# Moving sums and a broadcast ahead of preparation products in TensorE's order in a selective-scan layer

## The chip, the cores and the metric

The kernel runs on one core of a Trainium2 chip. The metric is the device time of one launch in microseconds (us), the median of a few runs. The core has five engines with a queue each: TensorE (PE, matmuls; its weight loads are listed as PEld), VectorE (DVE), ScalarE (ACT), GpSimd (POOL) and SyncE (SP, which here issues nearly all transfers). Each runs its own list of instructions and waits on semaphores for the others. A smaller time is better.

## The reference

Four layers are applied to an image batch of 3 x 256 x 48 x 48 in float32, each as `x = x + layer(group_norm(x))`: an attention block, a convolution with routed weights, a plain 3 x 3 convolution, and a selective scan (Mamba) layer. The change is in the scan layer alone. For every batch and token it computes, cut to what matters:

```python
xn = layer_norm(x)                          # over the 256 channels
u  = silu(causal_conv4(in_proj_x(xn)))      # 512 channels
z  = in_proj_z(xn)                          # 512 channels
dt_raw, B, C = split(x_proj(u), [16, 16, 16])
dt = softplus(dt_proj(dt_raw))
h  = h * exp(dt * A) + dt * B * u           # 512 channels x 16 states, token after token
y  = sum_over_states(h * C) + u * D
out = out_proj(y * silu(z))
```

## The kernel before

The 2304 tokens of each of the three batches are cut into six chunks of 384 tokens (`CH`), so the scan layer has 18 chunks (`todo`), taken one after the other. A chunk has 512 x 16 = 8192 rows of state, which are run as eight **steps** (m, h): m = 0..3 names a block of 128 channels, h = 0, 1 the half of the states. A step has eight **parts**, each a scan of 128 rows over 384 tokens. Part p of a step is written "p0" to "p7" below, with the step before it: (1,0) p3.

What one part does: ACT computes `exp(A * dt)` into one of three PSUM slots (`decay`, L1758), and DVE runs the recurrence in place over a buffer `hs` (`scan`, L1766). The decay of a part is issued three parts ahead, into the slot that the scan just listed has freed. So ACT can be at most three parts ahead of DVE, and whatever else is listed on ACT between two decays delays those behind it.

What a step needs besides: the buffer `hs` is filled with `dt * B * u` beforehand, the upper half by DVE from PSUM (`fill_upper`, L1719), the lower by POOL from SBUF (`fill`, L1733). After the step's eight scans, POOL multiplies the states by C (`times_c`, L1783), and one step later PE sums them over the states into the PSUM tile `ps_y` (`add_states`: eight matmuls of 32 columns, L1800, and with h = 0 one matmul with the diagonal of D ahead of them, L1795, which opens a new `ps_y`). `gate` on DVE (L1807) multiplies the finished `ps_y` by silu(z). It stands at the end of step (m,1) for block m-1, and `ps_y` has one buffer, so the opening matmul of `add_states` at the end of (m,1) needs that gate. `dt * u` reaches the scans in two ways: `spread_pe` (L1689, four listed matmuls) broadcasts it over partitions into the PSUM tile `ps_r`, which has one buffer and is read by `fill_upper`; `spread` reads it and dt back from DRAM through SP's queue into the SBUF tiles `dtur` and `dtr`.

Beside the scans of chunk `at`, the next chunks are prepared. This work is laid out by hand in the table `plan`: an entry (j, place, rel, stage) puts a stage of chunk at + rel into half-step j = 0..15 of chunk `at` (j = 4m + 2h, plus 1 for parts 4 to 7). The places are points in the order of listing: MID after the second part of the half-step, DONE after the third, LATE after the fourth, and PE_ for TensorE's products: for an even j after part p3, for an odd j after the whole step. `keep_order` makes PE, DVE, ACT and POOL execute exactly in the order of listing.

The preparation shares two PSUM banks (`bank[0]`, `bank[1]`), and its order is:

- j = 0, 1, 3, 4 (PE_): `taps` 0 to 3, the products of the convolution, 16 matmul instructions each (L1264), into banks 0, 1, 0, 1; `take_u` (ACT, L1273) empties them at MID of j = 2, 3, 5, 6.
- j = 3 and j = 7 (LATE): `silu` of z and of u on ACT, each with a table load before and after (L1278, L228).
- j = 5 and 6 (PE_): `project_y` 0 and 1 of the chunk before (L1353, L1355); `store` (ACT copy L1365, then a DMA) empties bank 0 at j = 6 LATE and bank 1 at j = 8 MID.
- j = 7 (PE_): `project_u` (L1284); j = 8 LATE: `take_dbc`.
- j = 8 and 10 (PE_): `project_dt` 0 and 2 (L1310); j = 9 and 11 LATE: `softplus` on ACT (L1319 to L1321); j = 10 and 12 MID: `take_dt` (four DVE instructions in place over the two banks and into `dtu`, L1326, L1327); j = 10 and 12 DONE: `keep_dt` (two ACT copies, L1331, that empty the banks, and two DMAs to DRAM).
- j = 12 (PE_): `less_mean` (L1222) of the chunk after the next; j = 13 LATE: `centre` (L1235, L1237); j = 13 (PE_): `square_mean` (L1229); j = 14 MID: `inverse_root` (L1241, L1242); j = 15 MID: `normalise` (DVE, L1246).
- j = 13 to 15 (PE_): `project_z` (L1341), emptied by `take_z` (ACT, L1349).

At the end of a step the list on PE was so far: the odd half-step's preparation product, then `add_states` of the step before, then, with h = 0, `spread_pe` for the step after the next.

Of the kernel before, what the change touches and what calls it, by code (L numbers as in the profile page):

```python
# [9 lines left out]
F32 = mybir.dt.float32  # L10
# [6 lines left out]
P = 128  # L17
# [8 lines left out]
CH = 384  # L26
# [57 lines left out]
def net(  # L84
# [295 lines left out]
    with ExitStack() as l0:  # L380
# [36 lines left out]
        with ExitStack() as p1:  # L417
# [15 lines left out]
            for b in ORDER:  # L433
# [3 lines left out]
                for ct in range(CT):  # L437
                    for j in range(parts):
                        at = slice(j * N // parts, (j + 1) * N // parts)
# [754 lines left out]
    def fetch(at):  # L1194
        k = chunks[at] = Chunk()
        k.at = at
        k.b, k.c = todo[at]
        k.before = chunks.get(at - 1)
        k.xg = room(k, "xg")
        nc.sync.dma_start(k.xg, xd[k.b][:, :, k.c * CH : (k.c + 1) * CH])  # L1200
# [106 lines left out]
    def project_dt(k, m0):  # L1307
        for j in range(2):
            m = m0 + j
            nc.tensor.matmul(  # L1310
                bank[j], w3v["dtsb"][:, m * P : (m + 1) * P], k.dbc[: DTR + 1, :],
                start=True, stop=True,
            )

    def softplus(k, m0):

        both = k.dt[:, m0 : m0 + 2, :]
        for j in range(2):
            nc.scalar.activation(k.dt[:, m0 + j, :], bank[j], AF.Abs)  # L1319
        nc.scalar.activation(both, both, AF.Exp, scale=-1.0)  # L1320
        nc.scalar.activation(both, both, AF.Ln, bias=1.0)  # L1321

    def take_dt(k, m0):
        for j in range(2):
            m, pdt = m0 + j, bank[j]
            nc.vector.scalar_tensor_tensor(pdt, pdt, 0.0, k.dt[:, m, :], ALU.max, ALU.add)  # L1326
            nc.vector.tensor_tensor(k.dtu[:, m, :], pdt, k.u[:, m, :], ALU.mult)  # L1327

    def keep_dt(k, m0):
        for j in range(2):  # L1330
            nc.scalar.copy(k.dt[:, m0 + j, :], bank[j])  # L1331
        if m0 == 0:
            k.dtd, k.dtud = {}, {}
        d = k.dtd[m0] = dram.tile([P, 2, CH], F32, name=f"dtd{m0}")
        nc.sync.dma_start(d, k.dt[:, m0 : m0 + 2, :])
        d = k.dtud[m0] = dram.tile([P // 2, 2, CH], F32, name=f"dtud{m0}")
        nc.sync.dma_start(d, k.dtu[P // 2 :, m0 : m0 + 2, :])
# [13 lines left out]
    def project_y(k, mo, lo=0, hi=DI):  # L1351
        if lo == 0:
            nc.tensor.matmul(bank[mo], ident, k.ot[:, mo, :], start=True, stop=False)  # L1353
        for m in range(lo, hi):
            nc.tensor.matmul(  # L1355
                bank[mo], w("out", m * 256 + mo * P, P), k.sz[:, m, :],
                start=False, stop=m == DI - 1,
            )
# [5 lines left out]
    def store(k, mo):  # L1364
        nc.scalar.copy(k.ot[:, mo, :], bank[mo])  # L1365
        nc.sync.dma_start(
            out[k.b, mo * P : (mo + 1) * P, k.c * CH : (k.c + 1) * CH], k.ot[:, mo, :]
        )
# [3 lines left out]
    MID, DONE, LATE, PE_ = range(4)  # L1372
# [18 lines left out]
        (8, LATE, 1, take_dbc),  # L1391
        (8, PE_, 1, lambda k: project_dt(k, 0)),
        (9, LATE, 1, lambda k: softplus(k, 0)),
        (10, MID, 1, lambda k: take_dt(k, 0)),
        (10, DONE, 1, lambda k: keep_dt(k, 0)),
        (10, PE_, 1, lambda k: project_dt(k, 2)),
        (11, LATE, 1, lambda k: softplus(k, 2)),
        (12, MID, 1, lambda k: take_dt(k, 2)),
        (12, DONE, 1, lambda k: keep_dt(k, 2)),
    ]  # L1400

    after = [
# [2 lines left out]
        (3, LATE, 0, lambda k: silu(k.sz)),  # L1405
        (2, MID, -1, residual),
        (5, PE_, -1, lambda k: project_y(k, 0)),
        (6, LATE, -1, lambda k: store(k, 0)),
        (6, PE_, -1, lambda k: project_y(k, 1)),
        (8, MID, -1, lambda k: store(k, 1)),  # L1410
    ]
# [10 lines left out]
    def run(at, j, place):  # L1422
        for when, where, rel, stage in after + plan + gating:
            if (when, where) == (j, place) and 0 <= at + rel < len(todo):
                stage(chunks[at + rel])
# [230 lines left out]
    with ExitStack() as l3:  # L1656
# [5 lines left out]
        scn = l3.enter_context(tc.tile_pool(name="scn", bufs=2, reuse_waits="tile"))  # L1662
# [10 lines left out]
        def spread(k, m):  # L1673

            dtr = scn.tile([P, 4, CH], F32, name="dtr")
            dtur = scn.tile([P, 2, 16 + CH], F32, name="dtur")[:, :, 8 : 8 + CH]
            for t, src in ((dtr, k.dtd), (dtur, k.dtud)):
                src = src[m & 2][:, m & 1, :]
                for i in range(4):
                    r = slice(32 * i, 32 * i + 32)  # L1680
                    nc.sync.dma_start(t[r], src.rearrange("(q d) n -> d q n", d=32))
            return dtr, dtur

        def spread_pe(k, m):

            t = psr.tile([P, 2, 512], F32, name="ps_r")
            for q in range(2):
                r = slice(32 * q, 32 * q + 32)
                nc.tensor.matmul(  # L1689
                    t[:, q, :CH], rep[r].rearrange("p r d -> p (r d)"), k.dtu[r, m, :],  # L1690
                    start=True, stop=True,
                )
            k.ps = t
# [69 lines left out]
        def scan(s, part):  # L1763
            g, q = parts_of_step[part]
            b = tiles[s][:, g, q, :]
            nc.vector.tensor_tensor_scan(  # L1766
                b, slots[(8 * s + part) % 3][:, : CH + 1], b, 0.0, ALU.mult, ALU.add
            )
# [42 lines left out]
        k = chunks[0]  # L1811
# [6 lines left out]
        for s, (at, m, h) in enumerate(steps):  # L1818
            if m == 0 and h == 1 and at + 2 <= last:
                fetch(at + 2)  # L1820
            for part in range(8):
                j = 4 * m + 2 * h + part // 4
                scan(s, part)
                decay(8 * s + part + 3)
                if part == 0 and h == 0:
                    c, n = (at, m + 1) if m + 1 < DI else (at + 1, 0)
                    if c <= last:
                        rows = getattr(chunks[c], "rows", {})
                        chunks[c].rows = {**rows, n: spread(chunks[c], n)}
                if part == 4 and s + 1 < len(steps):  # L1830
                    first_states(s + 1)
                if part % 4 == 1:
                    run(at, j, MID)
                if part % 4 == 2:
                    run(at, j, DONE)
                if h == 1 and part == 7 and s >= 3:
                    gate(*steps[s - 3][:2])
                if part % 4 == 3:
                    run(at, j, LATE)
                if part == 3:  # L1840
                    run(at, j, PE_)
            if s + 1 < len(steps):
                fill(s + 1)
            last_states(s)
            times_c(s)
            run(at, 4 * m + 2 * h + 1, PE_)
            if s >= 1:
                add_states(s - 1)

            if h == 0 and s + 2 < len(steps):  # L1850
                spread_pe(chunks[steps[s + 2][0]], steps[s + 2][1])

        end = len(steps) - 1
        k = chunks[last]
# [122 lines left out]
```

## Time and profile before

| What | Value |
|---|---|
| median of three runs | 3452.4 us (3451.87 to 3458.52) |
| profiled execution, time | 3452.73 us |
| its span | 3451.2 us |
| scans, first to last start | 2025.8 to 3428.7 us |
| busy over the span: PE, DVE, ACT, POOL | 90%, 85%, 68%, 41% |
| granted TensorE clock, mean | 0.944 |

The scan stage fills the last two fifths of the span. POOL is nearly idle before it and nearly always busy in it, so its 41% says little; the stage is to be read by itself. One chunk takes 78.5 us there, and the order repeats from chunk to chunk: `normalise` is at 2650.26 us in one chunk and at 2728.69 us in the next. Within a line of the timeline the columns are the start in us, the length in us, engine, source line, operation, output and inputs, how many instructions were merged, and in brackets the idle time ahead of them with what ended it. Neighbouring instructions of one engine overlap a little in these records (a scan lasts 0.93 us but follows the one before after 0.85 us), so distances between starts are used where a queue is counted.

### The profile page before, as it was taken

The page shows a single profiled execution, that of the slowest core. Times are in us where ns is not written, and L with a number is a line of the kernel's source. Part 1 is how long each engine was busy: PE and PEld are TensorE (multiplying, and loading weights), DVE is VectorE, ACT ScalarE, POOL GpSimd, SP SyncE. Part 2 cuts the span into 40 slices and gives each one's busy share as a digit, 9 for nine tenths or more (in the row PEclk, how much of TensorE's full clock was granted, in tenths as well). Part 3 has the DMA queues.
Part 4 walks back from the last instruction along what each step waited for, and adds up shares of the span by engine and source line. Part 5 has one row for each costly group of instructions (what it writes and reads, how often), then busy time and mean ns, then how long its engine had stood idle before and what let it go on. Part 6 is the DMA issues. An engine that isn't in the chain of part 4 may idle for free. (4 is left out here: it accounts for less than half of the span.)

```text
span 3451.2 us, 51999 instructions
## 1 busy us (share of the span) xinstructions
PE 3115.5 (90%) x20170; PEld 1496.8 (43%) x20170; DVE 2937.4 (85%) x3306; ACT 2353.3 (68%) x3508; POOL 1430.3 (41%) x385
## 2 busy tenths in 40 slices
PE   7999999999999999879999988888888888888885
PEld 4334343443433335457677753333344443333331
DVE  4799899859899994589965379999999999999998
ACT  3788888748888884422224467777777777777774
POOL 0000000000000001110000059999999999999997
PEclk9999999999999999999999998889999999988987
DMA  4000000010000003756302134444544444544441
GB/s 178 14 8 10 8 10 8 8 42 5 11 6 8 10 8 112 240 190 222 133 22 67 46 97 115 109 105 114 120 102 115 102 109 113 119 114 107 116 111 43
DMA packets 167603, 273.95 MB, mean 79 GB/s; under 512 B 30049, under 2 KB 134561, under 8 KB 165426
## 3 DMA queue, kind: packets, MB, share of 16 engines
q1 hardware_dynamic: 154114, 250.48, 26.9%
q10 hardware_dynamic: 13232, 20.06, 1.8%
q8 instruction: 160, 2.62, 0.3%
q14 instruction: 97, 0.79, 0.1%
HBM read 223.12 MB, written 47.10 MB: 78 GB/s over the span
## 5 line engine op out<-in xcount | busy, mean ns | idle before, releaser
L641 ACT ACTIVATE pt<-ps_s 128x1024 f32<-128x1024 f32 x972 | 942.4, 1022 | 154.7 <-PE ps_s L637 142.1
L1766 DVE TENSOR_TENSOR_SCAN hs<-ps_da,hs 128x385 f32<-128x385 f32 x1152 | 1003.9, 937 | 30.7 <-ACT ps_da L1758 27.3
L856 DVE TENSOR_TENSOR part<-part,pt 128x2048 f32<-128x2048 f32 x396 | 906.7, 2290 | 41.2 <-ACT pt L641 18.4
L1758 ACT ACTIVATE ps_da<-dtr,u 128x384 f32<-128x384 f32 x1152 | 656.5, 583 | 244.1 <-DVE hs L1766 225.9
L163 POOL TENSOR_TENSOR rstd<-ve,mhalf 128x2 f32<-128x2 f32 (+1 forms) x26 | 16.4, 631 | 1475.9 <-DVE ve L161 1475.9
L637 PE MATMUL ps_s<-q,kt 32*128 32x512 f32 (+1 forms) x4320 | 576.4, 592 | 0.1
L650 PE MATMUL acc<-pt,vt 128*32 128x512 f32 (+1 forms) x4320 | 520.9, 561 | 0.2
L1783 POOL TENSOR_TENSOR hc<-hs,x 128x3072 f32<-128x3072 f32 x72 | 445.6, 6188 | 18.9 <-DVE hs L1766 16.0
L1513 PE MATMUL ps_c<-vt,u 128*128 128x288 f32 x1728 | 432.7, 411 | 20.5 <-DVE u L262 20.5
L1783 POOL TENSOR_TENSOR hc<-hs,bc 128x3072 f32<-128x3072 f32 x71 | 437.8, 6166 | 17.3 <-DVE hs L1766 15.1
L1264 PE MATMUL ps_g<-u 128*128 128x384 f32 x1152 | 388.6, 492 | 7.4 <-ACT sz L1349 3.2
L1513 PEld LDWEIGHTS ps_c<-vt,u 128*128 128x128 f32 x1728 | 330.7, 192 | 117.1 <-issue 18.8
L1264 PEld LDWEIGHTS ps_g<-u 128*128 128x128 f32 x1152 | 214.8, 190 | 180.3 <-ACT ps_da L1758 19.3
L637 PEld LDWEIGHTS ps_s<-q,kt 32*128 32x128 f32 x4320 | 195.2, 183 | 199.1 <-issue 120.2
L1800 PE MATMUL ps_y<-hc,u 128*32 128x384 f32 x2304 | 245.0, 548 | 19.6 <-POOL hc L1783 19.1
L1733 POOL TENSOR_TENSOR hs<-dtur,x 128x1536 f32<-128x1536 f32 x72 | 248.9, 3457 | 6.3 <-DMA dtur<-dtud 6.3
L1733 POOL TENSOR_TENSOR hs<-dtur,bc 128x1536 f32<-128x1536 f32 x72 | 248.5, 3451 | 0.0
L650 PEld LDWEIGHTS acc<-pt,vt 128*32 128x32 f32 x4320 | 94.4, 108 | 353.4 <-issue 326.7
L1310 PE MATMUL ps_g<-wconv,u 17*128 17x384 f32 x144 | 79.2, 684 | 85.0 <-ACT x L1331 85.0
L1800 PEld LDWEIGHTS ps_y<-hc,u 128*32 128x32 f32 x2304 | 64.2, 117 | 177.8 <-issue 143.1
L1222 PE MATMUL ps_g<-wconv,u 128*128 128x384 f32 x144 | 80.3, 725 | 62.1 <-ACT x L1331 62.1
L321 POOL MEMSET xpad<- 128x212 f32 x12 | 5.7, 472 | 313.4 <-ACT xpad L1564 234.9
(246 smaller groups left out, 3624.0 us busy)
## 6 DMA issues: line engine op xcount, KB each, us to landing
wconv<-in_we SPq DMA_DIRECT2D x144, 384.0 KB, 4.2
dtr<-dtd SPq DMA_DIRECT2D x288, 192.0 KB, 3.9
dtur<-dtud SPq DMA_DIRECT2D x288, 96.0 KB, 4.2
wconv<-xd SPq DMA_DIRECT2D x36, 384.0 KB, 4.3
x<-bcd SPq DMA_DIRECT2D x72, 192.0 KB, 6.0
dtd<-x SPq DMA_DIRECT2D x36, 384.0 KB, 3.1
bc<-bcd SPq DMA_DIRECT2D x72, 192.0 KB, 6.0
yc<-ycat ACTq DMA_DIRECT2D x18, 576.0 KB, 4.7
```

The source lines that it names most:

```text
L637: nc.tensor.matmul(s[:, j, cols], kt[r, mt * P : (mt + 1) * P], q[r, :n], start=True, stop=True,)
L641: nc.scalar.activation(p[:, h0 : h0 + 2, :], s, AF.Exp)
L650: nc.tensor.matmul(acc[h * HD : (h + 1) * HD, :n], vt[:, mt, g * P + h * HD : g * P + (h + 1) * HD], p[:, h, cols], start=mt == 0, stop=mt ...
L856: ): nc.vector.tensor_tensor(part, first, p, ALU.add)
L1222: nc.tensor.matmul(bank[to], w3v["less"][:, int(to != ct), :], k.xg[:, ct, :], start=ct == 0, stop=ct == CT - 1,)
L1264: nc.tensor.matmul(bank[m % 2], w3v["wtap"][:, tap, ct, m * P : (m + 1) * P], k.xn[:, ct, tap : tap + CH], start=tap == 0 and ct == 0, sto ...
L1513: nc.tensor.matmul(pc[:, :HN], u[:, i, dy, ct, m * P : (m + 1) * P], vt[:, i, ct, dy * TW : dy * TW + HN], start=ct == 0 and dy == 0, stop ...
L1733: nc.gpsimd.tensor_tensor(states(s)[:, :, 2:4, 1:], chunks[at].rows[m][1].unsqueeze(1).broadcast_to([P, 2, 2, CH]), b_rows(s, 0, 2), ALU.mult,
L1758: nc.scalar.activation(slots[n % 3][:, 1 : CH + 1], chunks[at].rows[m][0][:, q, :], AF.Exp, scale=amat[:, col : col + 1],)
L1766: nc.vector.tensor_tensor_scan(b, slots[(8 * s + part) % 3][:, : CH + 1], b, 0.0, ALU.mult, ALU.add)
L1783: nc.gpsimd.tensor_tensor(hc, tiles[s][:, :, :, 1:], cb.broadcast_to([P, 2, 4, CH]), ALU.mult)
L1800: nc.tensor.matmul(k.y_ps[32 * q : 32 * q + 32, :CH], fold, hc[:, g, q, :], start=False, stop=h == 1 and g == 1,)
```

## The change

Four edits, all in the scan layer:

- At the end of a step, `add_states` and `spread_pe` are listed before the odd half-step's preparation product instead of after it.
- `take_dt` goes from MID to DONE of j = 10 and 12 (one part later), and `keep_dt` from DONE to LATE (one part later).
- `store(k, 0)` goes from LATE of j = 6 to MID of j = 7 (two parts later).
- The SBUF tile `dtur` loses 16 padding elements per row and its offset of 8 elements.

```diff
-        (10, MID, 1, lambda k: take_dt(k, 0)),
-        (10, DONE, 1, lambda k: keep_dt(k, 0)),
+        (10, DONE, 1, lambda k: take_dt(k, 0)),
+        (10, LATE, 1, lambda k: keep_dt(k, 0)),
         (10, PE_, 1, lambda k: project_dt(k, 2)),
         (11, LATE, 1, lambda k: softplus(k, 2)),
-        (12, MID, 1, lambda k: take_dt(k, 2)),
-        (12, DONE, 1, lambda k: keep_dt(k, 2)),
+        (12, DONE, 1, lambda k: take_dt(k, 2)),
+        (12, LATE, 1, lambda k: keep_dt(k, 2)),
...
         (5, PE_, -1, lambda k: project_y(k, 0)),
-        (6, LATE, -1, lambda k: store(k, 0)),
+        (7, MID, -1, lambda k: store(k, 0)),
...
-            dtur = scn.tile([P, 2, 16 + CH], F32, name="dtur")[:, :, 8 : 8 + CH]
+            dtur = scn.tile([P, 2, CH], F32, name="dtur")
...
             times_c(s)
-            run(at, 4 * m + 2 * h + 1, PE_)
             if s >= 1:
                 add_states(s - 1)
-
             if h == 0 and s + 2 < len(steps):
                 spread_pe(chunks[steps[s + 2][0]], steps[s + 2][1])
+            run(at, 4 * m + 2 * h + 1, PE_)
```

## The prediction

> **What bounds the kernel now.** I read first the busy times of one chunk's stretch of the scan stage, then DVE's waits, then the timelines of DVE, ACT and PE over that chunk. The busy times, one stretch (PE, PEld, DVE, ACT, POOL):
>
> ```profile
> 2636.40:2715.00 78.60, 66.47 (x280) 30.88 (x280) 75.52 (x90) 61.69 (x120) 76.39 (x17) 0.89 0.46 111
> ```
>
> DVE and POOL are both nearly full: 75.5 and 76.4 of 78.6 us. A chunk cannot get shorter than POOL's 76.4 us, about 2 us below now, and what DVE loses to waits is all there is to win. DVE's waits over sixteen chunks (2150 to 3400 us), with totals, times and longest:
>
> ```profile
> DVE hs L1766 <- ACT ps_da L1758: 24.2, 32, 0.9
> DVE ps_g L1326 <- ACT x L1321: 10.0, 16, 0.6
> DVE hs L1719 <- PE ps_r L1689: 4.0, 15, 0.3
> ```
>
> With 3.2 + 2.9 us at the gates (L1807) that is 44 us, some 2.8 us a chunk. The timeline places them. DVE, one chunk:
>
> ```profile
> 2649.38 0.96 DVE L1766 TENSOR_TENSOR_SCAN hs<-ps_da,hs 128x385 f32<-128x385 f32 x1 [0.81 <-ACT ps_da L1758]
> ...
> 2670.76 0.56 DVE L1807 TENSOR_TENSOR sz<-ps_y,sz 128x384 f32<-128x384 f32 x1 [0.40 <-PE ps_y L1800]
> 2671.59 2.62 DVE L1719 TENSOR_TENSOR hs<-ps_r,x 128x1536 f32<-128x1536 f32 x2 [0.27 <-PE ps_r L1689]
> 2674.13 6.90 DVE L1766 TENSOR_TENSOR_SCAN hs<-ps_da,hs 128x385 f32<-128x385 f32 x8
> ...
> 2688.59 0.96 DVE L1766 TENSOR_TENSOR_SCAN hs<-ps_da,hs 128x385 f32<-128x385 f32 x1 [0.75 <-ACT ps_da L1758]
> ...
> 2702.55 0.57 DVE L1326 SCALAR_TENSOR_TENSOR ps_g<-ps_g,x 128x384 f32<-128x384 f32 x1 [0.63 <-ACT x L1321]
> ```
>
> They are: (3,1) p5, behind the variance chain; the gate and the fill at the end of (0,1); (1,1) p7, behind `store`; and `take_dt` in (2,1). The change aims at the last four, 0.40 + 0.27 + 0.75 + 0.63 = 2.05 us a chunk. Now PE, where the order changes:
>
> ```profile
> 2640.09 4.66 PE L1222 MATMUL ps_g<-wconv,u 128*128 128x384 f32 x8 [3.89 <-ACT x L1331]
> 2646.20 1.56 PE L1229 MATMUL ps_g<-wconv,mean 128*128 128x384 f32 x4 [1.44 <-ACT wconv L1237]
> ...
> 2658.68 10.59 PE L1264 MATMUL ps_g<-u 128*128 128x384 f32 x32 [0.38 <-ACT x L1349]
> 2669.20 1.50 PE L1800 MATMUL ps_y<-hc,u 128*32 128x384 f32 x16
> 2670.62 0.91 PE L1689 MATMUL ps_r<-x,u 32*128 32x384 f32 x4
> 2671.47 5.43 PE L1264 MATMUL ps_g<-u 128*128 128x384 f32 x16
> ```
>
> From 2658.68 us PE runs with no gap shown: taps 0 and 1 (32 instructions), sums, spread, taps 2. Over the whole chunk PE has 12 us idle, but none here. And ACT, which waits for those products:
>
> ```profile
> 2669.30 0.58 ACT L1273 ACTIVATE u<-ps_g,vec 128x384 f32<-128x384 f32 x1
> 2669.78 1.20 ACT L1758 ACTIVATE ps_da<-dtr,u 128x384 f32<-128x384 f32 x2
> 2671.00 1.28 ACT L1278 ACT_TABLE_LOAD   x1
> 2672.29 1.48 ACT L1278 ACTIVATE x<-x 128x1536 f32<-128x1536 f32 x1
> 2673.80 1.28 ACT L228 ACT_TABLE_LOAD   x1
> 2675.09 0.20 ACT L1748 COPY hst<-hs 128x8 f32<-128x8 f32 x1
> 2675.20 0.58 ACT L1758 ACTIVATE ps_da<-dtr,u 128x384 f32<-128x384 f32 x1
> ...
> 2687.59 0.48 ACT L1365 COPY wconv<-ps_g 128x384 f32<-128x384 f32 x1 [1.66 <-PE ps_g L1355]
> ```
>
> `take_u(1)` starts 0.1 us after the last of taps 1, and behind it stand two decays, the whole silu of z, and the decay of (1,0) p3.
>
> **The change part by part.** Times are those of this chunk; a shift is what DVE runs later than before.
>
> *A, sums and spread before taps 1.* Sums and spread take 2.27 us of PE (2671.47 - 2669.20). Their inputs are there: POOL's product for them ran 2653.08 to 2659.23, and `ps_r` is free when the fill at 2662.61 ends. So they run right after taps 0, the gate (0.40) and the fill (0.27) wait no more, and taps 1 ends 2.27 later. `take_u(1)` then starts at 2669.30 + 2.27 = 2671.57. From its start to the end of the p3 decay is 2675.20 + 0.58 - 2669.30 = 6.48 us, so that decay ends at 2678.05. DVE's scan p3 stood at 2674.13 + 3 x 0.85 = 2676.69; without the two waits it wants to start at 2676.02 and waits 2.07. Shift: 2.07 - 0.67 = +1.40. The two waits are won, and a longer one takes their place three scans later.
>
> *B, store two parts later.* At the end of (0,1) the sums, now first, need the gate, which ends at 2670.9; PE is with taps 1 until 2671.5, so no gap opens. Taps 2 and 3 are both ahead of the next pair of sums and spread; PE stays gapless, and `project_y(0)`, now behind that pair, ends 2.27 us later. The copy can start at 2687.59 + 2.27 = 2689.86. ACT reaches its new place, after the decay that follows (1,1) p5, at about 2689.0, so it still waits, 0.9 instead of 1.66. From the copy's start to the end of the decay of (2,0) p3 were 7.38 us (2694.97 - 2687.59), four decays among them; two of these, 0.52 each, are now ahead of the copy: 6.34. That decay ends at 2696.20; the scan stood at 2692.45 + 2.56 = 2695.01. The wait of 0.75 at (1,1) p7 goes, but the shift after (2,0) p3 is +1.2, whatever A left.
>
> *C, take_dt one part later.* In (2,1) ACT's softplus ends at 2702.5 and DVE waited 0.63. One scan (0.85) now lies before: the wait goes, -0.63, shift +0.6. In (3,0) there was none.
>
> *D, keep_dt one part later, and sums and spread before the variance product.* `less_mean` waits for `keep_dt`'s copies, which come one scan later: +0.85. Behind `less_mean` PE was idle for 1.44 us, waiting for `centre`; sums and spread now use that and overrun by 2.27 - 1.44 = 0.83, and 0.11 comes back since `square_mean` took 1.56 us after the idle time and four such matmuls take 1.45 without it. `inverse_root` and the decay of p5 behind it follow `square_mean`: +0.85 + 0.72 = +1.57 on the wait of 0.81 at (3,1) p5. No cover: DVE already waits there. The chunk's shift is +0.6 + 1.57 = +2.2.
>
> *E, the way back.* In (3,1) the sums now stand before `project_z` 2 and 3 and wait for the gate, 0.59 us after its start (as 2710.39 - 2709.80 shows elsewhere). Sums and products, 2.2 + 2.8, end 5.6 us after the gate's start; `take_z` of the second bank stood 5.8 after it (2658.6 - 2652.8). It holds by 0.2, so taps 0 keeps its place against DVE and the shift carries over to the next chunk. PE is idle for about 2.0 us ahead of these sums, instead of 0.6 ahead of the products. The nearest row, 1.44 us of idle time, cost 0.11 on four matmuls; the far one, 3.89, made `less_mean` 4.66 us for eight where eight `project_y` matmuls run 2.74: +1.9. I take the near one, which the 0.2 covers; 0 to 1.9 is kept for the range. The page "TensorE: Matmul & The Clock Gate" of the Trainium skill, section "What's actually happening", says the array drops to half clock after an idle window of about 3.4 us. By it 2.0 us mostly cost nothing, and the sum below would stand as it is; by the far row, which lies past that window, it would be some 30 us more.
>
> *F, dtur and the queues.* The fills on POOL now last 3.42 to 3.53 us. Only their row pitch changes. With chunks of 80.7 us POOL has over 4 us to spare, 0.5 a fill; shorter fills win nothing. I cost it at 0. `dtur`'s DMA lands 4.2 us after its issue and is wanted a step later. On SP's queue nothing stands between the old and the new places of the `store` and `keep_dt` DMAs; dt's write comes about 1 us later, `spread` reads it at the next step's start, some 5 us on, and its write lands in 3.1. That is covered.
>
> *Sum.* Fifteen chunks of 2.2: 33. The first chunk has no `project_y`: there the spread must wait for the fill at 2033.9, taps 1 comes behind it, cold, 7.5 to 8 us (a cold taps took 8.05), `take_u(1)` falls to about 2044.3, and with the same 6.5 us the decay of (1,0) p3 is ready at 2050.8 against a scan at 2047.1: +3.6; with C and D +4.3. Chunk 17 of 18 has A to C alone: +0.6. The last has no preparation, and DVE waits there on POOL. Together +37.5 us on the profiled 3452.73: 3490 us. The profiled run lies 0.3 above the median.
>
> **The rivals.**
>
> *Faster: the later products are hidden.* If ACT took up the delay of taps 1, all four waits would go: 2.05 us, capped by POOL at about 2.0, over 16 chunks -32: 3420. For it: ACT is idle for 17 us of a chunk. Against it: before (1,0) p3 ACT has 0.9 us of slack (decay ready at 2675.78, scan at 2676.69), of which the removed waits eat 0.67; the delay must be below 0.24 us, and it is 2.27.
>
> *Small loss: D is hidden.* If `keep_dt` still came in time (the copies need only that `take_dt` is done) and sums and spread fitted the idle time, only A to C count: 17 x 0.6 and the first chunk's 3: +13, 3466. Against it: the copies stand behind one more decay in ACT's order.
>
> *Larger loss: the clock.* The far row of E in each chunk: 2.2 + 1.9, 16 times: +66 to 70, 3520.
>
> *Nothing moves.* If PE took another order than listed, or fills got so much shorter as to balance it. `keep_order` speaks against the first, POOL's slack against the second.
>
> **How the numbers follow.** Likeliest case 0.74, own range 3476 to 3506 (a chunk's shift between 1.4 and 3.2, from C's and E's bounds); small loss 0.09; larger loss 0.06; faster 0.08; nothing 0.03. A median here tells 0.2%, 7 us, from no change. Faster 0.08, same 0.03, slower 0.89. The range, 3463 to 3510, takes in the small loss and part of the larger.
>
> **What would show it.** A: waits at the gate and the fill in (0,1) gone, one of about 2 us on L1758 at (1,0) p3, ACT waiting some 2.2 us at L1273. B: none at (1,1) p7, about 0.5 to 0.7 at (2,0) p3, and ACT waiting 0.9 at L1365. C: L1326's wait near 0. D: about 1.0 at (3,1) p3 and 1.6 at p5; PE's wait before L1229 gone. DVE's waits 5 us a chunk, a chunk 80.7 us. I am wrong if a chunk stays below 78.5, which needs taps 1 to end where it does now.

## The result and the profile after

The changed kernel takes 3508.8 us (median of four runs, 3507.2 to 3514.8) against 3452.5 us before (median of four): 1.0162 times as long, with a 95% interval from 1.0145 to 1.018. That is 56 us more. The forecast was 3490 us with a range of 3463 to 3510: the sign was right, the size fell 19 us short, and the result lies 1.2 us below the upper end of the range, beyond the 3476 to 3506 us given for the likeliest case.

The profiled execution took 3509.1 us, its span 3507.3 us. The 56.1 us more of its span come apart by the start of the scans and by the starts of `normalise` (L1246), of which there is one in each of sixteen chunks:

| Part | Before | After | Difference |
|---|---|---|---|
| first scan starts at | 2025.81 | 2028.46 | +2.7 |
| from there to the first `normalise` | 74.37 | 75.66 | +1.3 |
| fifteen chunks, `normalise` to `normalise` | 1178.02 | 1227.78 | +49.8 (a chunk: 78.53 to 81.85, +3.32) |
| from the last `normalise` to the end | 173.0 | 175.4 | +2.4 |

The first row is no effect of the change: nothing ahead of the scans was touched, and over the profiled runs of this study that start lies anywhere from 2022.3 to 2032.0 us. Nearly all of the rest is 3.3 us a chunk.

The busy times of one chunk of the kernel after (stretch, its length, PE, PEld, DVE, ACT, POOL, granted clock, DMA share, GB/s):

```profile
2654.10:2736.30 82.20, 69.41 (x282) 31.84 (x283) 76.63 (x91) 62.94 (x124) 77.86 (x17) 0.85 0.46 110
```

DVE and POOL work about as long as before, and the chunk is longer around them. DVE's largest wait of the kernel after, over the same stretch of time as in the kernel before, 2150 to 3400 us or some sixteen chunks (total, times, longest):

```profile
DVE hs L1766 <- ACT ps_da L1758: 97.7, 72, 2.3
```

The gate, the fill and `take_dt` no longer wait; the waits of the scans for their decays went from 24.2 to 97.7 us, and those three had cost 20 together. The timeline of DVE in the kernel after places them, from (3,1) of one chunk through the whole of the next to (0,0) p5 of the one behind it:

```profile
2672.84 1.81 DVE L1766 TENSOR_TENSOR_SCAN hs<-ps_da,hs 128x385 f32<-128x385 f32 x2 [0.97 <-ACT ps_da L1758]
2676.22 0.96 DVE L1766 TENSOR_TENSOR_SCAN hs<-ps_da,hs 128x385 f32<-128x385 f32 x1 [1.57 <-ACT ps_da L1758]
...
2697.11 0.53 DVE L1807 TENSOR_TENSOR sz<-ps_y,sz 128x384 f32<-128x384 f32 x1
2697.56 2.61 DVE L1719 TENSOR_TENSOR hs<-ps_r,x 128x1536 f32<-128x1536 f32 x2
...
2704.99 4.36 DVE L1766 TENSOR_TENSOR_SCAN hs<-ps_da,hs 128x385 f32<-128x385 f32 x5 [2.26 <-ACT ps_da L1758]
...
2723.20 4.36 DVE L1766 TENSOR_TENSOR_SCAN hs<-ps_da,hs 128x385 f32<-128x385 f32 x5 [0.64 <-ACT ps_da L1758]
2730.88 0.54 DVE L1326 SCALAR_TENSOR_TENSOR ps_g<-ps_g,x 128x384 f32<-128x384 f32 x1
...
2757.58 0.96 DVE L1766 TENSOR_TENSOR_SCAN hs<-ps_da,hs 128x385 f32<-128x385 f32 x1 [1.57 <-ACT ps_da L1758]
2769.36 2.66 DVE L1766 TENSOR_TENSOR_SCAN hs<-ps_da,hs 128x385 f32<-128x385 f32 x3 [1.02 <-ACT ps_da L1758]
```

In order: (3,1) p3 and p5; the gate and the fill at the end of (0,1), without a wait; (1,0) p3 with 2.26 us, three scans behind them; (2,0) p3 with 0.64; `take_dt` in (2,1) without a wait; the next chunk's (3,1) p5; and a wait that the forecast's sum did not have, 1.02 us at (0,0) p5. It stands in 11 of the 16 chunks. ACT in the kernel after, the three rows behind these waits:

```profile
2698.61 0.58 ACT L1273 ACTIVATE u<-ps_g,vec 128x384 f32<-128x384 f32 x1 [2.50 <-PE ps_g L1264]
...
2716.89 0.48 ACT L1365 COPY wconv<-ps_g 128x384 f32<-128x384 f32 x1 [0.96 <-PE ps_g L1355]
...
2768.36 0.48 ACT L1349 COPY sz<-ps_g 128x384 f32<-128x384 f32 x1 [0.81 <-PE ps_g L1341]
```

`take_u(1)` waits 2.5 us for taps 1, `store` 0.96 for `project_y`, and `take_z` (L1349) in (0,0) waits for its product, which it did not before. PE in the kernel after shows why:

```profile
2666.13 4.70 PE L1222 MATMUL ps_g<-wconv,u 128*128 128x384 f32 x8 [4.70 <-ACT x L1331]
...
2690.87 1.50 PE L1800 MATMUL ps_y<-hc,u 128*32 128x384 f32 x16
2692.30 0.92 PE L1689 MATMUL ps_r<-x,u 32*128 32x384 f32 x4
2693.14 5.43 PE L1264 MATMUL ps_g<-u 128*128 128x384 f32 x16
...
2761.60 1.23 PE L1795 MATMUL ps_y<-x,diag 128*128 128x384 f32 x2 [2.04 <-DVE x L1807]
2762.76 2.79 PE L1800 MATMUL ps_y<-hc,u 128*32 128x384 f32 x16
2765.48 2.85 PE L1341 MATMUL ps_g<-u 128*128 128x384 f32 x8
```

Sums and spread, 2.27 us from start to start, stand right ahead of taps 1, which ends that much later. At the end of (3,1) PE is idle 2.04 us for the gate, as forecast, but the sixteen sums behind it then take 2.79 us where they take 1.50 at the full clock. The busy times of three neighbouring stretches of the kernel after, columns as above, show the clock there:

```profile
2758.70:2762.00 3.30, 1.26 (x4) 0.49 (x3) 3.30 (x5) 2.77 (x8) 1.24 (x2) 1.00 0.62 152
2762.10:2765.40 3.30, 3.30 (x18) 0.59 (x16) 3.30 (x4) 1.46 (x4) 3.30 (x1) 0.50 1.07 225
2765.50:2768.80 3.30, 3.30 (x14) 1.98 (x11) 2.84 (x4) 1.56 (x5) 3.30 (x2) 1.00 0.34 85
```

After a stretch with PE busy 1.26 of 3.30 us, the clock is granted at half for one stretch, and the sums lie in it. Below, "cold" stands for matmuls at the half clock and "warm" for those at the full one. How long PE was busy does not decide it alone. More stretches of the same kernel, the first ahead of the same sums one chunk earlier:

```profile
2676.80:2680.10 3.30, 1.40 (x4) 0.52 (x4) 3.30 (x5) 2.77 (x7) 1.71 (x2) 1.00 0.43 124
...
2806.50:2809.80 3.30, 2.60 (x11) 0.98 (x13) 3.30 (x5) 3.20 (x8) 3.30 (x2) 1.00 0.23 75
2809.90:2813.20 3.30, 3.30 (x20) 0.94 (x12) 3.30 (x5) 3.00 (x6) 3.30 (x2) 0.50 0.84 214
```

Behind 1.40 us of work the clock stays full, and the sums take 1.50 us after the same 2.04 us of idle time. Behind 2.60 us of it, among them the narrow matmuls of `project_dt` (17 rows), it drops to half. What the clock answers to is not settled here.

### The profile page after: what moved, and what is told of

The parts are those of the page before. It is cut to its first block, busy times and chain, and to the rows that moved or that the text cites. A ratio compares the mean times of both kernels' runs of the same rounds, so it can differ in the third digit from the quotient of the medians.

```text
span 3507.3 us, 52039 instructions
## 1 busy us (share of the span) xinstructions
PE 3152.9 (90%) x20170; PEld 1505.9 (43%) x20170; DVE 2934.7 (84%) x3306; ACT 2351.8 (67%) x3508; POOL 1432.5 (41%) x385
## 5 line engine op out<-in xcount | busy, mean ns | idle before, releaser
L1800 PE MATMUL ps_y<-hc,u 128*32 128x384 f32 x2304 | 264.7, 586 | 22.8 <-POOL hc L1783 22.4
```

The lines of the kernel that those rows point to most:

```text
L1800: nc.tensor.matmul(k.y_ps[32 * q : 32 * q + 32, :CH], fold, hc[:, g, q, :], start=False, stop=h == 1 and g == 1,)
```

## The experiments

Each of the twelve kernels was compared with the kernel before on the same chip; a ratio stands with its 95% interval. Two numbers of each trace do the work: DVE's waits in one chunk, and the length of a chunk from `normalise` to `normalise`.

**The parts alone.** First the new order of PE without the three other edits:

```diff
             times_c(s)
-            run(at, 4 * m + 2 * h + 1, PE_)
             if s >= 1:
                 add_states(s - 1)
             if h == 0 and s + 2 < len(steps):
                 spread_pe(chunks[steps[s + 2][0]], steps[s + 2][1])
+            run(at, 4 * m + 2 * h + 1, PE_)
```

> Before, with the new order on TensorE alone (sums and spread ahead of the product of every odd half-step; take_dt, keep_dt, store and dtur as before). Theory L (late products hold up ACT, and the decays behind them on ACT come late): project_y(0) ends some 2.4 us later and store's copy, still ahead of four decays, passes all of it on (+2.4 a chunk); the variance product costs 0.8 more at (3,1) p5; the wait at (0,0) p5 that the changed kernel shows is there in most chunks (+0.7). Together +3.5 to 4 a chunk, some 3508 to 3515 us: the order alone is as dear as the whole change. Rival K (the loss is that of keep_dt one part later, the order itself gains the waits at the gate and the fill, 0.67 a chunk): 3441 us. Rival S (dtur's layout): 3452 us.

Measured: 3534.0 us, 1.0230 (1.021 to 1.0249). The order alone costs more than the whole change, 79 us against 56, and more than was expected. Two rows of DVE in this kernel, (1,0) p3 and (1,1) p7:

```profile
2629.92 4.36 DVE L1766 TENSOR_TENSOR_SCAN hs<-ps_da,hs 128x385 f32<-128x385 f32 x5 [2.32 <-ACT ps_da L1758]
2642.81 0.96 DVE L1766 TENSOR_TENSOR_SCAN hs<-ps_da,hs 128x385 f32<-128x385 f32 x1 [1.73 <-ACT ps_da L1758]
```

The first is the wait of the forecast. The second is `store` in its old place, where it now waits 2.66 us for `project_y(0)`, which the sums have pushed back. So the loss is the order's, and the three other edits take a part of it back: together they are worth some 24 us (1.0230 against 1.0162). The later `store` takes 1.73 us at (1,1) p7 away for 0.63 at (2,0) p3.

Then the later `take_dt` and `keep_dt` alone, at both places:

```diff
-        (10, MID, 1, lambda k: take_dt(k, 0)),
-        (10, DONE, 1, lambda k: keep_dt(k, 0)),
+        (10, DONE, 1, lambda k: take_dt(k, 0)),
+        (10, LATE, 1, lambda k: keep_dt(k, 0)),
...
-        (12, MID, 1, lambda k: take_dt(k, 2)),
-        (12, DONE, 1, lambda k: keep_dt(k, 2)),
+        (12, DONE, 1, lambda k: take_dt(k, 2)),
+        (12, LATE, 1, lambda k: keep_dt(k, 2)),
```

> Before, with take_dt and keep_dt one part later at both places, nothing else. Theory L: -0.63 a chunk at take_dt in (2,1), +0.85 at (3,1) through less_mean and the variance chain: +0.2 a chunk, 3452 to 3457 us. Rival K: the whole loss, about 3500 us.

Measured: 3454.7 us, 0.9995 (0.9985 to 1.0005), no difference. The 0.63 us at `take_dt` are gone and a new wait stands ahead of the old one in (3,1), in DVE's timeline of this kernel:

```profile
2650.39 1.81 DVE L1766 TENSOR_TENSOR_SCAN hs<-ps_da,hs 128x385 f32<-128x385 f32 x2 [0.78 <-ACT ps_da L1758]
2653.02 0.96 DVE L1766 TENSOR_TENSOR_SCAN hs<-ps_da,hs 128x385 f32<-128x385 f32 x1 [0.81 <-ACT ps_da L1758]
```

Then `store` alone, and the tile `dtur` alone:

```diff
-        (6, LATE, -1, lambda k: store(k, 0)),
+        (7, MID, -1, lambda k: store(k, 0)),
```

> Before, with store(k, 0) two parts later, nothing else. Theory L: project_y(0) ends where it did, so ACT no longer waits for it and DVE's wait of 0.75 at (1,1) p7 goes without a new one: 17 times 0.75, 3440 us. Rival (the silu of u behind it comes as late as before, or the two banks' order makes a new wait): 3452 us.

```diff
-            dtur = scn.tile([P, 2, 16 + CH], F32, name="dtur")[:, :, 8 : 8 + CH]
+            dtur = scn.tile([P, 2, CH], F32, name="dtur")
```

> Before, with dtur without padding and offset, nothing else. Theory L: no difference, 3452 us, POOL's fills 3.42 to 3.53 us as before. Rival S: the layout carries the loss or a part of it, 3460 to 3508 us, to be seen in the length of the fills or in dtur's landing.

Measured: `store` 3454.2 us, 0.9997 (0.9987 to 1.0006), where a gain was expected; `dtur` 3453.1 us, 0.9997 (0.9988 to 1.0007), with POOL's fills at 3.41 to 3.50 us. In the kernel with the later `store`, DVE's wait of 0.75 us at (1,1) p7 is gone and this stands right behind it, at the end of (1,1):

```profile
2690.13 0.56 DVE L1807 TENSOR_TENSOR x<-ps_y,x 128x384 f32<-128x384 f32 x1 [0.37 <-PE ps_y L1800]
2690.96 2.62 DVE L1719 TENSOR_TENSOR hs<-ps_r,x 128x1536 f32<-128x1536 f32 x2 [0.27 <-PE ps_r L1689]
```

DVE came 0.75 us earlier to a gate for which PE had the sums only behind a product: 0.64 of the 0.75 went there. The 0.11 us that should be left do not show either: a chunk stays at 78.5 us.

**What of the +3.3 us belongs to E.** E is the forecast's step on the sums of (3,1). In the kernel after they run cold, wholly or in part (2.38 to 2.79 us), in 11 of 16 chunks. Two ways to avoid that were tried. The first keeps the order of before at j = 15 alone:

```diff
             times_c(s)
+            odd = 4 * m + 2 * h + 1
+            sums_first = odd != 15
+            if not sums_first:
+                run(at, odd, PE_)
             if s >= 1:
                 add_states(s - 1)
             if h == 0 and s + 2 < len(steps):
                 spread_pe(chunks[steps[s + 2][0]], steps[s + 2][1])
-            run(at, 4 * m + 2 * h + 1, PE_)
+            if sums_first:
+                run(at, odd, PE_)
```

> The changed kernel, with the old order at j = 15 alone (project_z 2 and 3 before the sums). The changed kernel shows a wait of about 1.03 us at (0,0) p5 in 11 of 16 chunks. Theory L: it comes from project_z ending late behind the sums, so here it is gone, 11 x 1.03: about 3497 us. Rival: it is a consequence of the chunk's other delays: no change, 3508 us.

The second keeps the new order and fills PE's idle time: the product `project_z(2, 0)` is issued there once more, ahead of the sums. It is work done twice, and its result is written again by the product in its own place.

```diff
             times_c(s)
+            if m == 3 and h == 1 and at + 1 < len(todo):
+                project_z(chunks[at + 1], 2, 0)
             if s >= 1:
                 add_states(s - 1)
```

> The changed kernel, with the product project_z(2, 0) issued once more ahead of the sums at j = 15, into the same bank, where its result is written again by the real one: TensorE is busy for 1.4 of the 2.04 us that it idles there. Theory clock: the sums and products behind the idle time run slow in 11 of 16 chunks because the array has cooled; here they run at the warm length, the wait at (0,0) p5 is gone with the order kept: about 3497 us. Rival order: the two matmul groups in a row are too long even warm, and more work makes it later: 3508 us or more.

Measured: 3506.8 us, 1.0148 (1.0131 to 1.0165), and 3509.7 us, 1.0161 (1.0144 to 1.0178). Some 12 us were expected of each, and neither gave them. PE in the kernel with the filler, the same sums:

```profile
2673.25 0.91 PE L1795 MATMUL ps_y<-u,diag 128*128 128x384 f32 x2
2674.09 1.50 PE L1800 MATMUL ps_y<-hc,u 128*32 128x384 f32 x16
```

They run warm, and the wait at (0,0) p5 is gone from those sixteen chunks of both kernels. So the cause of that wait is shown: the half clock behind the idle time. But the time does not follow. DVE in the kernel with the old order at j = 15, (3,1) p3 and p5:

```profile
2675.01 1.81 DVE L1766 TENSOR_TENSOR_SCAN hs<-ps_da,hs 128x385 f32<-128x385 f32 x2 [1.75 <-ACT ps_da L1758]
2678.69 0.96 DVE L1766 TENSOR_TENSOR_SCAN hs<-ps_da,hs 128x385 f32<-128x385 f32 x1 [1.88 <-ACT ps_da L1758]
```

What left (0,0) came back in (3,1): 1.75 and 1.88 us in the place of 1.20 and 1.58 in the mean of the kernel after. The waits are 6.5 us a chunk there and 6.4 after, and a chunk settles at 81.92 us in both kernels. PE in the kernel with the old order at j = 15 shows where the time went, and the two lengths are the same in the one with the filler:

```profile
2667.52 5.49 PE L1222 MATMUL ps_g<-wconv,u 128*128 128x384 f32 x8 [4.70 <-ACT x L1331]
2672.94 1.80 PE L1800 MATMUL ps_y<-hc,u 128*32 128x384 f32 x16
```

`less_mean` takes 5.49 us in every settled chunk, against 4.69 to 5.30 (4.95 in the mean) in the kernel after, and the sums behind it 1.80 against 1.50. These 0.54 and 0.30 us match the 0.55 and 0.30 more that DVE waits at p3 and p5. What was saved at (0,0) is lost again at half clock. How it settles is worth a look; the lengths of successive chunks of the kernel with the old order at j = 15 are 81.24, 81.58, 81.69, 81.80, 81.84, 81.90, 81.91, 81.92, 81.92, 81.92.

**One place of the order alone.** The sums ahead of taps 1, at j = 1, in the kernel before:

```diff
+            odd = 4 * m + 2 * h + 1
+            sums_first = odd == 1
```

with the branches of the diff above around the sums.

> Before, with sums and spread ahead of taps 1 only (j = 1), all else as before. Theory L: the waits at gate and fill in (0,1) go (-0.67 a chunk), one of 2.3 us comes at (1,0) p3, project_y(0) ends when it did, so the wait of 0.75 at (1,1) p7 goes since DVE is late anyway: net +0.85 to 0.9 a chunk, about 3469 us. Rival K (sums first gain their 0.67): 3442 us.

Measured: 3473.6 us, 1.005 (1.0033 to 1.0066), close to the 3469 us expected. DVE in this kernel, (1,0) p3:

```profile
2613.49 4.36 DVE L1766 TENSOR_TENSOR_SCAN hs<-ps_da,hs 128x385 f32<-128x385 f32 x5 [2.26 <-ACT ps_da L1758]
```

The gate and the fill in (0,1) wait no more and this wait of 2.26 us stands in their place: step A of the forecast is shown by itself. It also takes the 0.75 us at (1,1) p7 away.

**take_dt back at j = 12 in the kernel after:**

```diff
-        (12, DONE, 1, lambda k: take_dt(k, 2)),
-        (12, LATE, 1, lambda k: keep_dt(k, 2)),
+        (12, MID, 1, lambda k: take_dt(k, 2)),
+        (12, DONE, 1, lambda k: keep_dt(k, 2)),
```

> The changed kernel, with take_dt and keep_dt at j = 12 put back to their old places. Theory L: less_mean starts one scan earlier, the waits at (3,1) p3 and p5 shrink by 0.85 together: 15 times, about 3496 us. Rival (the variance chain is late through the sums ahead of it alone): 3508 us.

Measured: 3505.1 us, 1.0144 (1.0127 to 1.0161); 3496 was expected. DVE's waits in a chunk are 0.91, 1.57, 1.00, 2.31 and 0.63, and the chunk is 81.92 us once more. The copies come a scan earlier (0.85 us), but `less_mean` takes 5.43 to 5.49 us once settled, 0.5 longer; p3 waits 0.91 instead of 1.20, p5 the same 1.57, and the wait of E, about 1.0 us, stands in all sixteen chunks instead of eleven.

**A better kernel, by the waits.** By the waits alone a combination should win: both remedies where DVE waited, on the kernel before, then the sums first where ACT has room, with `take_u(1)` moved out of the way. The first has `store` later and `take_dt` later at j = 10 alone:

```diff
-        (10, MID, 1, lambda k: take_dt(k, 0)),
-        (10, DONE, 1, lambda k: keep_dt(k, 0)),
+        (10, DONE, 1, lambda k: take_dt(k, 0)),
+        (10, LATE, 1, lambda k: keep_dt(k, 0)),
...
-        (6, LATE, -1, lambda k: store(k, 0)),
+        (7, MID, -1, lambda k: store(k, 0)),
```

> Before, with take_dt and keep_dt one part later at j = 10 only, and store(k, 0) two parts later; TensorE's order as before. Expected: the wait of 0.63 at take_dt in (2,1) goes; store alone moved its wait of 0.75 into 0.37 at the gate and 0.27 at the fill of (1,1), 0.11 is won. 17 times 0.74: 12.5 us less, ratio 0.9964. Rival: the 0.63 is also only moved: ratio 0.9995 to 1.

The second adds the sums ahead of taps 1 (`sums_first = odd == 1`, as above) and

```diff
-        (3, MID, 1, lambda k: take_u(k, 1)),
+        (4, MID, 1, lambda k: take_u(k, 1)),
```

> As the run with take_dt at j = 10 and store moved, and besides sums and spread ahead of taps 1 (j = 1 only) with take_u(1) moved behind the silu of z (from MID of j = 3 to MID of j = 4), so that no decay waits for taps 1. Theory L with TensorE's gapless run as the bound: the waits at gate and fill in (0,1), 0.67, go, but the sums at the end of (1,0) stay where TensorE has them, and the wait at the gate of (1,1) grows by the same: ratio as without it, 0.9964. Rival (ACT alone is the bound): 0.67 more a chunk, ratio 0.993.

Measured: 3452.8 us, 0.9998 (0.9989 to 1.0007), and 3450.7 us, 0.9990 (0.9981 to 0.9999). Both missed the 0.9964 expected of them. In the second the gate and the fill in (0,1) wait no more, and the gate of (1,1) waits 0.94 us instead of 0.36, as its theory had it. DVE in the kernel with the two remedies, (3,1) p3 and p5:

```profile
2647.62 1.81 DVE L1766 TENSOR_TENSOR_SCAN hs<-ps_da,hs 128x385 f32<-128x385 f32 x2 [0.81 <-ACT ps_da L1758]
2650.24 0.96 DVE L1766 TENSOR_TENSOR_SCAN hs<-ps_da,hs 128x385 f32<-128x385 f32 x1 [0.81 <-ACT ps_da L1758]
```

The 0.63 us are won in (2,1) and 0.81 are paid in (3,1), where the copies for `less_mean` come no later than before. PE in this kernel:

```profile
2640.22 5.39 PE L1222 MATMUL ps_g<-wconv,u 128*128 128x384 f32 x8 [4.39 <-ACT x L1331]
```

`less_mean` was 4.54 to 4.71 us in the settled chunks of the kernel before. Warm, the same eight matmuls take 2.75 to 2.85 us (below). The clock says why. Busy times of neighbouring stretches of one chunk of the kernel before (in 8 of the fifteen chunks from `normalise` to `normalise` the three short ones are all at half clock):

```profile
2705.30:2715.40 10.10, 7.29 (x22) 2.26 (x22) 10.07 (x13) 8.17 (x17) 10.10 (x3) 0.50 0.49 121
2715.50:2718.80 3.30, 0.16 (x1) 0.16 (x2) 3.27 (x6) 2.13 (x5) 3.30 (x2) 1.00 0.00 0
2718.90:2722.20 3.30, 3.30 (x6) 1.74 (x6) 3.30 (x5) 2.69 (x7) 1.57 (x2) 0.50 0.74 222
2722.30:2783.70 61.40, 55.40 (x253) 26.44 (x251) 58.47 (x69) 48.33 (x93) 61.13 (x13) 1.00 0.48 110
```

and of the kernel with the two remedies:

```profile
2628.40:2635.10 6.70, 5.95 (x18) 2.27 (x22) 6.70 (x8) 5.90 (x13) 6.70 (x3) 0.50 0.61 153
2635.20:2638.50 3.30, 0.63 (x8) 0.00 (x0) 3.23 (x7) 2.40 (x4) 3.30 (x1) 1.00 0.00 0
2638.60:2645.30 6.70, 5.08 (x8) 2.53 (x8) 6.70 (x9) 4.71 (x10) 5.68 (x3) 0.50 0.61 157
2645.40:2706.80 61.40, 54.73 (x251) 26.39 (x250) 58.41 (x69) 48.94 (x93) 60.33 (x13) 1.00 0.46 108
```

In both the granted clock changes only at multiples of one length: the stretches are 3, 1, 1 and 18 times 3.413 us in the first, 2, 1, 2 and 18 times in the second (their ends are cut by 0.1 us here, so that each holds one state). A chunk is 23 of them in both, 78.50 us. `less_mean` falls into the last stretch at half clock and ends shortly after it: in the kernel before it starts 3.65 us ahead of that stretch's end (2718.64 to 2722.29) and takes 4.54; in the other it starts 5.17 us ahead of it (2640.22 to 2645.39) and takes 5.39. It comes 1.52 us earlier against the clock's steps and is 0.85 longer.

**The clock taken on directly.** If the half clock holds the chunk, matmuls that keep PE busy ahead of `less_mean` should set it free. Products with a tile of zeros, which add nothing to `ps_y`, do that. (A listed float32 product stands as two instructions in the records: the four of `less_mean` as x8, seven products with zeros as x14, the two of `spread_pe` as x4.) First three of them behind the sums of (2,1), on the kernel with the two remedies:

```diff
+        nil = wp.tile([P, P], F32, name="nil")
+        nc.vector.memset(nil, 0.0)
...
                 add_states(s - 1)
+            if m == 2 and h == 1 and at + 2 < len(todo):
+                k = chunks[at]
+                for _ in range(3):
+                    nc.tensor.matmul(
+                        k.y_ps[:, :CH], nil, k.u[:, m, :], start=False, stop=False
+                    )
```

> As the run with take_dt at j = 10 and store moved, and besides three products with a matrix of zeros added to the open sums in ps_y at the end of (2,1), in the 3.9 us in which TensorE idles ahead of less_mean. Theory clock: less_mean, 4.66 us for eight instructions behind the idle time, falls to about 3 us, the variance chain comes 1.5 us earlier and the wait of 0.81 at (3,1) p5 goes: 15 times 0.8 less, ratio 0.993. Rival (the length of less_mean is not from the idle time, or the products run into keep_dt's end and delay it): ratio 0.9964 or above.

Measured: 3452.6 us, 0.9996 (0.9987 to 1.0005), another miss. PE and DVE in this kernel:

```profile
2639.96 2.85 PE L1222 MATMUL ps_g<-wconv,u 128*128 128x384 f32 x8 [2.39 <-ACT x L1331]
2645.46 2.93 PE L1229 MATMUL ps_g<-wconv,mean 128*128 128x384 f32 x4 [2.65 <-ACT wconv L1237]
```

```profile
2650.01 0.96 DVE L1768 TENSOR_TENSOR_SCAN hs<-ps_da,hs 128x385 f32<-128x385 f32 x1 [1.77 <-ACT ps_da L1760]
```

`less_mean` fell from 5.39 to 2.85 us, as meant. But then PE is idle for 2.65 us behind it, `square_mean` is the cold one (2.93 in place of 1.56), and the whole wait stands at p5, 1.77 in place of 0.81 + 0.81. So it is in 14 of 16 chunks. In the other two `square_mean` takes 1.56 and p5 waits 0.40, but the gate in (0,1) has waited 1.33 instead of 0.40 in the same chunk. The chunk is 78.52 us in the mean.

The last run keeps PE busy on both sides. Against the kernel with the sums first at j = 1 it takes the sums first at j = 13 as well, and has fourteen products with zeros, seven ahead of the sums at the end of (2,0) and seven behind those of (2,1):

```diff
-            sums_first = odd == 1
+            sums_first = odd in (1, 13)
             if not sums_first:
                 run(at, odd, PE_)
+            if m == 2 and h == 0 and at + 2 < len(todo):
+                for _ in range(7):
+                    nc.tensor.matmul(
+                        chunks[at].y_ps[:, :CH], nil, chunks[at].u[:, m, :],
+                        start=False, stop=False,
+                    )
             if s >= 1:
                 add_states(s - 1)
...
             if sums_first:
                 run(at, odd, PE_)
+            if m == 2 and h == 1 and at + 2 < len(todo):
+                for _ in range(7):
+                    nc.tensor.matmul(
+                        chunks[at].y_ps[:, :CH], nil, chunks[at].u[:, m, :],
+                        start=False, stop=False,
+                    )
```

> Before, with take_dt and keep_dt at j = 10 one part later, store two parts later, sums first at j = 1 (take_u(1) behind the silu) and at j = 13, and seven products with a matrix of zeros added to ps_y ahead of the sums at the end of (2,0) and seven behind those at the end of (2,1), so that TensorE is not idle for long anywhere in a chunk. The runs so far settle on chunks of 78.50 or 81.92 us, whatever waits are taken out, and 81.92 - 78.50 = 3.42 us is the length of the shortest records of the granted clock (3.413): 23 and 24 of them. Theory W: a chunk's length is held at whole clock windows because less_mean and the chain behind it run at half clock up to a window's end; with the clock at full throughout, the hold is gone and a chunk takes what its waits leave, 75.7 + 1.4 = 77.1 us, POOL's 76.6 allowing: 15 x 1.4 less, some 3430 us, ratio 0.993. Rival P (POOL or another engine holds the chunk at 78.5): ratio 0.999 as without the zero products. Rival: the zero products themselves run into less_mean: above 1.

Measured: 3440.3 us (median of six, 3437.3 to 3444.3), 0.9967 (0.9955 to 0.9979): shorter than both kernels, by half of what was expected. PE in this kernel, ahead of and behind `less_mean`:

```profile
2627.87 4.78 PE L1866 MATMUL ps_y<-u,nil 128*128 128x384 f32 x14
2632.49 2.75 PE L1222 MATMUL ps_g<-wconv,u 128*128 128x384 f32 x8
...
2637.89 1.56 PE L1229 MATMUL ps_g<-wconv,mean 128*128 128x384 f32 x4 [0.38 <-ACT wconv L1237]
```

and its DVE and the clock there:

```profile
2641.06 0.96 DVE L1768 TENSOR_TENSOR_SCAN hs<-ps_da,hs 128x385 f32<-128x385 f32 x1 [0.40 <-ACT ps_da L1760]
```

```profile
2623.90:2627.20 3.30, 3.07 (x14) 1.10 (x18) 3.30 (x4) 2.92 (x6) 3.30 (x2) 0.50 0.18 54
2627.30:2702.30 75.00, 69.79 (x304) 34.04 (x300) 73.09 (x88) 59.87 (x117) 73.97 (x16) 1.00 0.49 117
```

The array runs warm through the whole variance chain, the wait at p5 is 0.40 in this chunk (1.45 in the one before, 0.88 in the mean), and a chunk takes 77.2 us in 7 of 15 cases and 77.7 to 78.3 in the others. PE works 6.2 us longer a chunk than in the kernel before (72.7 of 77.6 us in the mean, against 66.4 of 78.5), and a chunk is 0.9 us shorter. The half clock is not gone: the seven chunks of 77.2 us have one stretch of 3.413 us at half, the eight longer ones two, with the same instructions in all of them. Which part of it is the products' and which the order's at j = 13 was not separated. Adding matmuls that compute nothing is a way to test the cause, and no more than that is claimed for it.

## Why the prediction was right, and where it was short

**A was right.** 2.07 us was forecast at (1,0) p3 (its own rows give 2678.05 - 2676.02 = 2.03), 2.29 measured, with the gate and the fill free; alone (the run with j = 1) it gave 2.26. ACT's wait at L1273 was to be 2.2 and is 2.5.

**B was right:** nothing at (1,1) p7, 0.63 at (2,0) p3 (0.5 to 0.7 was said), 0.96 at L1365 (0.9). A and B together give 2.29 + 0.63 - 0.40 - 0.27 - 0.75 = +1.50 a chunk; the forecast had 1.2. **C was right** to the hundredth, -0.63. **D was right in kind and 0.4 small:** 1.20 in the mean at (3,1) p3 and 1.58 at p5, against "about 1.0 at p3 and 1.6 at p5", so 2.78 - 0.81 = +1.97 where +1.57 was taken. 0.3 of the 0.4 is the clock again: `less_mean` takes 4.95 us in the mean of fifteen chunks where it took 4.64 before, and the forecast left its length as it was. The wait of PE before L1229 is gone, as forecast. **F was right** for `dtur`, shown by its own run; the queues were not tested by themselves.

**E failed**, and it is the step of the forecast that did. It said that PE would be idle for 2.0 us ahead of the sums of (3,1) and that `take_z` holds by 0.2 us, so it cost nothing, with 0 to 1.9 kept as the bounds. The idle time is 2.04. But 0.76 us of idle time stand shortly ahead of it, and in 11 of 16 chunks the two fall so across the stretches of the clock that the sums meet the half clock. In the chunk shown the opening matmuls and the sums took 1.23 + 2.79 us instead of 0.91 + 1.50, 1.6 longer: 1.03 us of wait in 10 of the 15 chunks from the first `normalise` to the last, 0.69 in the mean. The near row was taken (0.11) where the far one (1.9) was closer. A nearer one stood in the trace of the kernel before: opening matmuls and sums at half clock took 1.65 + 2.79 us at the end of (2,1) (2710.39 and 2711.97 us). The page "TensorE: Matmul & The Clock Gate" of the Trainium skill, section "What's actually happening", was cited for a drop after an idle window of about 3.4 us. Its length of a window, 3413 ns, is the one seen in this trace; a window without any work is not what came ahead of the half clock here, since PE was busy for 1.26 of 3.30 us in it. The reading that the forecast took from the page, that 2.0 us mostly cost nothing, is refuted for this place: they cost nothing in 5 chunks and 1.0 us in 11.

The terms of the tally are then 1.50 - 0.63 + 1.97 + 0.69 = +3.5, against 3.3 measured and 2.2 forecast. Of the 1.4 us by which the tally is above the forecast, 0.7 is E's, 0.4 D's and 0.3 A's and B's. **The runs say that such a tally does not tell what taking one wait away is worth.** With the wait of E gone (two runs) or D's copies a scan earlier (one run), the chunk stayed at 81.92 us, and what was saved came back at another place, behind a `less_mean` that ran colder. The lengths show a pattern: 78.50 us is 23 times 3.413 and 81.92 is 24 times. The kernel before and six of its variants are at the first; the kernel after (327.68 us for four chunks, 96 stretches) and its three variants at the second. If a chunk is held at such lengths, a loss of 2.2 us by the waits becomes 3.41, one whole stretch of the clock, and the forecast's sum lacked the step from the one to the other: 15 x 3.41 = 51 against its 33, where 49.8 was measured. The other misses are smaller and one is of the other sign: the first chunk cost 1.3 and not 4.3, since A's wait there is 2.89 for 0.37 before (+2.5, not +3.6), D gave +0.7, and two other waits, of 0.59 and 1.23 us, went away; the tail cost 2.4 and not 0.6, with one of E's waits (1.03) in it. That the sum of all this still lies in the range is in part luck: 1.2 us more would have been outside it, and its upper end had been set by the larger loss.

What is shown here: that the lengths stay put while single waits come and go, that `less_mean` takes longer when it comes earlier against the clock's steps, in two of the runs by enough, with the sums behind it, to take back what was saved, and that with fourteen products more and one more change of order, which leave less of the half clock, the length moves. What is argued: that this is why they stay put. If of 1.52 us of earlier arrival 0.85 are lost again, each chunk hands about half of its lead to the next, and the loop settles where a chunk fits whole stretches. The lengths of the successive chunks of the run with the old order at j = 15 look so: their distance to 81.92 shrinks from 0.68 over 0.34 and 0.23 to 0.12, to a half or two thirds each time. It isn't settled why some kernels settle on a pattern over several chunks and not on one length: the order alone takes 83.12 and 84.13 in turn (167.25, 49 stretches), the one with j = 1 alone repeats over four chunks (317.5, 93 stretches), the last one likewise (310.6, 91).

**The rivals.** Faster (3420) fell as argued: ACT had 0.9 us of slack and taps 1 came 2.3 late. The larger loss by the clock (3520) named the right mechanism and the right place, in 11 chunks of 16 instead of all, and with 1.0 us of wait instead of 1.9. The small loss (3466) fell with the 2.0 us of D. "Nothing moves" fell with the waits at the places that A to D named.

## What to carry to other kernels

Here a tally of waits on the busiest engine gave the sign of the change and two thirds of its size, while savings of 0.6 to 0.8 us a chunk that it promised for other kernels did not come at all. Before such a tally is multiplied by the number of turns of a loop, compare the loop's length with the length of the stretches in which the granted clock changes. If it is a whole multiple of them and stays so from turn to turn, as here, a saving or a loss below one stretch may vanish or grow to a whole one, and a step that idles TensorE ahead of a chain of waits is the place to look. And work put ahead in an in-order queue delays what it passes by its whole length: here 2.27 us against 0.67 us of wait won, unless the engine behind has that much slack.

## What was not expected of the hardware

- The length of a turn of the loop sits on multiples of 3.413 us, the step of the granted clock: 78.50 us in seven kernels and 81.92 in four, to within 0.03 us in the mean of the settled chunks, while their waits differ by up to 1.0 us in a place. In the kernel after, single chunks lie between 81.36 and 82.26 us; three more kernels repeat over two or four chunks.
- The half clock came behind a stretch in which TensorE was busy for 38% of the time (1.26 of 3.30 us), and nearly doubled sixteen small matmuls from 1.50 to 2.79 us. It stayed away behind 1.40 of 3.30 us in the chunk before, and came behind 2.60 of 3.30 us at another place.
- Fourteen matmuls that compute nothing shortened a chunk, together with one change of order, by 0.9 us of 78.5.
- The row pitch of the tile that POOL's fills read (1600 or 1536 bytes) made no difference: 3.42 to 3.53 us a fill with the one, 3.41 to 3.50 with the other, three longer ones of some 120 aside in either kernel.
